# Another order of the pieces of an iteration in the chosen-token attention

## The chip, the core and the metric

The kernel runs on one core of one Trainium2 chip. The metric is the device time of one execution in microseconds. TensorE (PE) multiplies, VectorE (DVE), ScalarE (ACT) and GpSimd (POOL) do the elementwise work, and SyncE (SP) issues most of the plain DMAs. Each engine takes its instructions in a fixed order that is settled when the program is built, and waits on semaphores for the others.

## The reference

The reference is a chain of four blocks on x of shape (8, 512, 256) in float32, each added to its input: a gated recurrence with an MLP, a mixture of experts, a gated delta rule, and an attention among the half of the tokens that a gate chooses. The change is in the last one, which computes for every one of the eight batches:

```python
gate = jax.nn.sigmoid((token_inputs @ Wg)[..., 0])
_, idx = jax.lax.top_k(gate, C)                      # C = 256 of 512 tokens
attn_in = jnp.take_along_axis(token_inputs, idx[..., None], axis=1)
q, k, v = attn_in @ Wq, attn_in @ Wk, attn_in @ Wv   # 16 heads of 16
attn = jax.nn.softmax(jnp.einsum('bqhd,bkhd->bhqk', q, k) / jnp.sqrt(jnp.float32(dh)), axis=-1)
o = jnp.einsum('bhqk,bkhd->bqhd', attn, v).reshape(B, C, D) @ Wo
out = out.at[jnp.arange(B)[:, None], idx].set(o * gate_sel[..., None])
```

token_inputs is the layer-normalised x, and out is added to x.

## The kernel before

chosen_attention (from L1100) is a pipeline over the eight batches in 13 iterations. In iteration n seven parts work on seven different batches; a part is a generator, and every `yield` ends a piece of it.

- norm(n+1), one piece: loads x and normalises it to z.
- place(n), six pieces: turns z (ptd, L122), multiplies it by the gate's weights (pgt, L1167), and then on VectorE, token by token, counts how many gates lie ahead (L1181 to L1186): the rank. The last piece casts the rank to row numbers (L1189), scatters z with four indirect DMAs from GpSimd's queue (placed, L1193), one behind the other as all write one buffer, and loads the first 256 rows as c on SP's queue (L1195).
- project(n-1), six pieces: turns c (pct, copied to cT by VectorE at L1208), four pieces of products for q and k (pqk, L1220, two banks of 512 columns for each), and the products for v (pv, L1231).
- maxima(n-2), six pieces: for each half of the queries two pieces of scores (sc, L1250), whose negated row maxima VectorE takes (L1252), and one that turns the maxima (pmx, L1256) and adds them to q (L1257).
- sums(n-3), six pieces: for each half of the heads two pieces of scores of the other orientation (st, L1271), whose exponentials ScalarE takes (L1274), and one of products with v (po, L1281), copied to o (L1282).
- finish(n-4), five pieces: the denominators (pden, L1292, spread by GpSimd at L1297), two pieces that turn their reciprocals and multiply o (pr, L1304; L1305), the product with Wo (pdy, L1311, copied to y at L1312), and the DMAs: y stored on SP's queue (L1314), and read back row by row with four indirect DMAs from GpSimd's queue (got, L1317).
- leave(n-5), one piece: adds the gathered rows times the gate to x on VectorE (L1324, four instructions) and stores the result on SP's queue (L1325).

Every piece of scores, sc or st, takes all four banks of the pool px (the banks of scores), so it can start only when VectorE or ScalarE has read what the piece of scores before it left there. The other products use the pools pf and pp, two banks each:

```python
pf = cx.enter_context(tc.tile_pool(name="d_pf", bufs=2, space=PSUM))
pp = cx.enter_context(tc.tile_pool(name="d_pp", bufs=2, space=PSUM))
px = cx.enter_context(tc.tile_pool(name="d_px", bufs=4, space=PSUM))
```

The order of the pieces within an iteration is a list of letters written out by hand (L1338); what is left of a part is finished at the iteration's end. The tile framework then schedules: an instruction may be placed earlier or later on its engine than the list has it, even in a neighbouring iteration, as long as its inputs allow it, so that the list steers the engines' orders and does not fix them.

Of the kernel before, what the change touches and what calls it, by code (L numbers as in the profile page):

```python
# [45 lines left out]
def block(ctx: ExitStack, tc: tile.TileContext, a: dict, out: bass.AP):  # L46
# [1053 lines left out]
    def chosen_attention():  # L1100
# [4 lines left out]
        with ExitStack() as cx:  # L1105
# [45 lines left out]
            def norm(b):  # L1151
                x = tk.tile([P, NT, D], F32, name=f"dx{b}", tag="x", bufs=8)
                nc.sync.dma_start(x, rows_of(xbufs[1][b]))
                z = tk.tile([P, NT, D], F32, name=f"dz{b}", tag="z", bufs=3)
                center(sm, x, z, f"d{b}")
                zs[b] = x, z
                yield
# [170 lines left out]

            parts = {"p": (place, 0), "s": (sums, 3), "m": (maxima, 2), "q": (project, 1), "f": (finish, 4), "l": (leave, 5)}
            for _ in norm(0):
                pass
            for n in range(B + 5):
                at_work = {k: part(n - lag) for k, (part, lag) in parts.items() if 0 <= n - lag < B}
                if n + 1 < B:
                    at_work["n"] = norm(n + 1)
                for k in "p s q l m f p s q f m f s f p s q m q p s q m p m s q p m n f".split():  # L1338
                    if k in at_work:
                        next(at_work[k], None)  # L1340
                for left in at_work.values():
                    for _ in left:
                        pass

    chosen_attention()


# [44 lines left out]
```

## Time and profile before

| | |
|---|---|
| Time before, median of 3 runs | 3373.59 us (3373.55 to 3381.02) |
| The profiled execution's own time | 3381.53 us |
| Its span | 3379.8 us |
| TensorE busy in the span | 3018.4 us, 89% |
| VectorE | 1900.5 us, 56% |
| ScalarE | 1548.0 us, 46% |
| GpSimd | 574.0 us, 17% |
| DMA, mean | 90 GB/s |
| Granted TensorE clock, mean of the span | 0.91 |
| chosen_attention, in the span | 2904 to 3379.8 us |

The page reports one execution. A group's line has the source line, the engine, the operation, what it writes and reads, how often, the busy time and the mean of one, and at the end the idle time of its engine just before it and what ended it. The shares in the table are means over four blocks with different limits; the last block alone has TensorE busy 372.1 of its 476 us. The profiled execution is 7.9 us longer than the median of the runs.

### The profile page before, as it was taken

Reading aid. Unit: us, or ns where it says so; the run is one execution under the profiler, and the core shown is the slowest. Engines: PE = TensorE matmul, PEld = TensorE weight load, DVE = VectorE, ACT = ScalarE, POOL = GpSimd, SP = SyncE. Lnnn points to the kernel's source line nnn. Section 1 sums busy time; section 2 is a strip of 40 time slices with the busy share of each in tenths; the row PEclk is TensorE's granted clock in tenths of the full one; section 3 lists DMA queues with packets and bytes.
Section 4 is the critical chain, followed back from the end, with each engine's and each line's share of the span. In section 5 each row is a group of like instructions: output and inputs, shape, how many; then the busy total and the mean of one; then the engine's idle time right before and its main releaser. Section 6 shows DMA issues by size and latency. Waiting matters only on the chain.

```text
span 3379.8 us, 59439 instructions
## 1 busy us (share of the span) xinstructions
PE 3018.4 (89%) x24662; PEld 2227.4 (66%) x24662; DVE 1900.5 (56%) x4415; ACT 1548.0 (46%) x2747; POOL 574.0 (17%) x629
## 2 busy tenths in 40 slices
PE   7999999979999999977899898898989999498887
PEld 3655555535999999973566666666666667365664
DVE  4555545534555555556467767767677664554432
ACT  3554442212333333325466666767666663233322
POOL 1000001320000111014122222312121110212111
PEclk8999998989999999998789898989989896698787
DMA  5000003220788888871000000000000000201111
GB/s 205 13 25 13 13 13 148 69 67 19 271 337 330 330 327 320 327 284 31 2 1 20 8 20 8 26 2 26 2 23 2 8 2 8 94 23 42 36 40 47
DMA packets 97133, 302.69 MB, mean 90 GB/s; under 512 B 12760, under 2 KB 79456, under 8 KB 87648
## 3 DMA queue, kind: packets, MB, share of 16 engines
q0 software_dynamic: 19440, 221.19, 17.4%
q1 hardware_dynamic: 68016, 68.44, 6.0%
q10 hardware_dynamic: 9408, 9.27, 0.8%
q8 instruction: 194, 3.18, 0.4%
q14 instruction: 75, 0.61, 0.1%
HBM read 248.79 MB, written 50.08 MB: 88 GB/s over the span
## 4 chain that ended last, share of the span: by engine, by line
PE 69%; DVE 12%; DMA 11%; issue 4%; ACT 2%; POOL 2%; SPq 0%; another core or an unknown queue 0%; ACTq 0%; POOLq 0%; DVEq 0%
PE p_r L444 13%; PE pc L681 8%; DMA zbuf<-bz,rows 5%; PE pp L304 3%; PE pk L746 3%; PE pj L399 3%; PE pyr L522 3%; PE pkq L950 3%; DMA w<-in_experts,wrow 2%; PE pf L394 2%; PE p_s L444 2%; PE py L1008 2%; PE st L1271 2%; PE pw L957 1%; DVE cy L685 1%
## 5 line engine op out<-in xcount | busy, mean ns | idle before, releaser
L444 PE MATMUL p_r<-zT,w 128*128 128x128 f32 x4544 | 533.0, 275 | 6.1 <-DMA w<-in_experts,wrow 5.5
L444 PEld LDWEIGHTS p_r<-zT,w 128*128 128x128 f32 x4544 | 525.0, 192 | 11.6 <-issue 7.1
L685 DVE SCALAR_TENSOR_TENSOR cy<-pc,conv,cy 128x509 f32<-128x509 f32 (+2 forms) x480 | 351.4, 740 | 139.7 <-ACT cy L683 134.6
L448 ACT ACTIVATE t_r<-p_r,w 128x128 f32<-128x128 f32 x568 | 170.9, 374 | 263.5 <-PE p_r L444 183.9
L444 PE MATMUL p_s<-sxT,shared_w 128*128 128x512 f32 x512 | 226.2, 603 | 22.1 <-DVE l_s L449 20.4
L444 PEld LDWEIGHTS p_s<-sxT,shared_w 128*128 128x128 f32 x512 | 98.1, 193 | 145.6 <-issue 106.3
L508 POOL DMA_INDIRECT w<-in_experts,wrow x71 | 66.8, 940 | 676.3 <-ACT sg_r L457 655.8
L449 DVE SCALAR_TENSOR_TENSOR l_r<-p_r,w,t_r 128x128 f32<-128x128 f32 x284 | 80.0, 344 | 175.7 <-PE p_r L444 175.7
L681 PE MATMUL pc<-cxT,wq 128*128 128x512 f32 x256 | 150.8, 714 | 15.0 <-DVE cy L685 12.9
L681 PE MATMUL pc<-cxT,wk 128*128 128x512 f32 x256 | 146.0, 665 | 6.1 <-DVE cy L685 3.7
L304 PE MATMUL pp<-hT,win 128*128 128x512 f32 x320 | 142.9, 598 | 0.2 <-ACT hT L126 0.2
L522 PE MATMUL pyr<-w,htr 128*128 128x256 f32 x568 | 136.0, 383 | 2.6 <-DVE htr L462 2.6
L683 ACT ACTIVATE cy<-pc,conv 128x512 f32<-128x512 f32 x160 | 108.4, 686 | 62.3 <-PE pc L681 61.0
L449 DVE SCALAR_TENSOR_TENSOR g_r<-p_r,w,t_r 128x128 f32<-128x128 f32 x284 | 79.9, 344 | 98.8 <-PE p_r L444 98.8
L746 PE MATMUL pk<-kq 128*128 128x256 f32 x512 | 130.2, 391 | 0.7 <-DVE NQ L748 0.4
L728 POOL TENSOR_TENSOR e<-le,g 128x512 f32<-128x512 f32 x64 | 66.3, 1042 | 364.2 <-DVE NQ L748 341.6
L748 DVE SCALAR_TENSOR_TENSOR NQ<-pk,nbk,e 128x256 f32<-128x256 f32 x256 | 110.0, 477 | 27.2 <-PE pk L746 26.8
L394 PE MATMUL pf<-hT,fc 128*128 128x512 f32 x256 | 121.5, 601 | 0.0
L457 ACT ACTIVATE sg_r<-g_r 128x512 f32<-128x512 f32 x71 | 44.8, 631 | 159.9 <-DVE g_r L455 159.9
L399 PE MATMUL pj<-pj,sT 128*128 128x256 f32 x512 | 113.1, 379 | 0.0
L522 PEld LDWEIGHTS pyr<-w,htr 128*128 128x128 f32 x568 | 103.6, 192 | 14.2 <-issue 2.7
L950 PEld LDWEIGHTS pkq<-state,kq 128*128 128x128 f32 x768 | 95.4, 197 | 24.2 <-DVE state L972 16.7
(393 smaller groups left out, 6179.0 us busy)
## 6 DMA issues: line engine op xcount, KB each, us to landing
zt<-zbuf SPq DMA_DIRECT2D x71, 128.0 KB
ybuf<-yt SPq DMA_DIRECT2D x71, 128.0 KB
zbuf<-zeros SPq DMA_DIRECT2D x11, 768.0 KB
x<-in_x SPq DMA_DIRECT2D x8, 512.0 KB
xbuf<-x SPq DMA_DIRECT2D x8, 512.0 KB
sx<-xbuf SPq DMA_DIRECT2D x8, 512.0 KB
xbuf<-sx SPq DMA_DIRECT2D x8, 512.0 KB
cx<-xbuf SPq DMA_DIRECT2D x8, 512.0 KB
```

The source lines that it names most:

```text
L304: TE.matmul(ps, win[:, k, m : m + P], hT[:, k, :], start=k == 0, stop=k == DK - 1)
L394: TE.matmul(ps, fc[:, k, f * P : (f + 1) * P], hT2[:, k, :], start=k == 0, stop=k == DK - 1)
L399: TE.matmul(ps, sT[:, f, t * P : (t + 1) * P], pj[:, f, :], start=f == 0, stop=f == 7)
L444: last_of[0] = TE.matmul(ps[:, f, :], wx[:, k, (f0 + f) * P : (f0 + f + 1) * P], xin[:, k, :], start=k == 0, stop=k == DK - 1)
L448: S.activation(t3[:, f, :], p3[:, f, :], AF.Identity, bias=b3[:, f0 + f : f0 + f + 1])
L449: V.scalar_tensor_tensor(t1[:, f, :], p1[:, f, :], b1[:, f0 + f : f0 + f + 1], t3[:, f, :], ALU.add, ALU.mult)
L522: last_of[0] = TE.matmul(ps, hT[:, f, :], w2[:, f, :], start=f == 0, stop=f == 3)
L681: TE.matmul(ps, w[:, k, n * P : (n + 1) * P], xT[:, k, :], start=k == 0, stop=k == DK - 1)
L685: V.scalar_tensor_tensor(y[:, j:], ps[:, : T - j], conv[:, at + n, 3 - j : 4 - j], y[:, j:], ALU.mult, ALU.add)
L746: TE.matmul(pk[:, j, :, :], kq[:, h + j, 0, ts], kq[:, h + j, :, ts], start=True, stop=True)
L748: V.scalar_tensor_tensor(NQ[:, :, t * HG + h + j, :], pk[:, j, :, :], s.nbk[:, t, h + j : h + j + 1], bc(e[:, h + j, :], 1, 2), ALU.mult, ...
L950: TE.matmul(ps[:, n, h, :], s.kq[:, h, n, ts], state[:, h, :], start=True, stop=True)
```

## The change

Only the list of letters changes (an added empty line above it moves the later lines by one). It has the same letters but for one q more: project has six pieces, and a seventh call finds it finished.

```diff
             for n in range(B + 5):
                 at_work = {k: part(n - lag) for k, (part, lag) in parts.items() if 0 <= n - lag < B}
                 if n + 1 < B:
                     at_work["n"] = norm(n + 1)
-                for k in "p s q l m f p s q f m f s f p s q m q p s q m p m s q p m n f".split():
+                for k in "p s q q m f q s f q p m f s s p m f s q p m n l q m p s q p m f".split():
                     if k in at_work:
                         next(at_work[k], None)
```

By the list, l (the adding of results) moves from the fourth place to the 24th, n (the norm) from the 30th to the 23rd, the pieces of project move forward, and between two pieces that use the banks of scores (m and s, other than their third and sixth pieces) stand other pieces with products: two q between the first s and the first m, f and q between that m and the next s, and so on. Place's second piece comes after four pieces of project. Finish's fourth piece (f, pdy) comes after the fourth piece of sums and the third of maxima.

## The prediction

> **What bounds the kernel now.** I read the waits of the last stage first, then the stage cut into its iterations, then one iteration in order of time. The change touches only chosen_attention, which runs from 2904 us to the end, 476 of 3379.8 us.
>
> The waits from 2904 us on (engine, line, what is waited for: total us, times, longest):
>
> ```profile
> DVE dx L1324 <- DMA got<-result,at: 104.2, 30, 14.8
> ...
> POOL got L1317 <- DMA result<-dy: 90.1, 7, 23.2
> ...
> PE sc L1250 <- DVE maxs L1252: 30.1, 8, 8.3
> ```
>
> VectorE stands 104.2 us in front of the additions of leave, until the gathers land; TensorE stands 30.1 us because VectorE has not released score banks. The stage in stretches from one gate product (pgt) to the next: the two starting iterations, iterations 4 to 7, then 8 and 9, which place nothing (columns: stretch, length, busy us of PE, PEld, DVE, ACT, POOL, then granted clock):
>
> ```profile
> 2952.00:3032.60 80.60, 71.90 (x439) 49.96 (x439) 45.04 (x105) 26.60 (x48) 12.00 (x12) 0.89 0.09 29
> 3032.60:3088.80 56.20, 46.03 (x298) 31.70 (x297) 23.65 (x52) 17.36 (x31) 10.22 (x11) 0.79 0.13 38
> ...
> 3140.90:3191.60 50.70, 44.60 (x297) 31.52 (x296) 22.45 (x48) 17.37 (x31) 10.28 (x11) 0.80 0.14 42
> ...
> 3240.90:3285.80 44.90, 41.45 (x288) 29.51 (x285) 15.31 (x26) 13.23 (x27) 4.98 (x6) 0.81 0.10 30
> 3285.80:3325.90 40.10, 34.15 (x242) 22.79 (x240) 14.87 (x26) 10.50 (x21) 4.97 (x6) 0.74 0.11 34
> ```
>
> TensorE is busy 44.6 of 50.7 us at a clock of 0.80, so it is not at its own limit. What sets the 50.7 us is in the iteration from 3140.9, in order of time:
>
> ```profile
> 3148.78 0.69 DVE L1252 TENSOR_REDUCE maxs<-sc 128x2 f32<-128x512 f32 x1
> ...
> 3156.62 0.17 DVE L1189 CAST at<-rank 128x4 int32<-128x4 f32 x1
> ...
> 3157.07 1.06 POOL L1193 DMA_INDIRECT placed<-dz,at  x1 [7.20 <-DVE rank L1190]
> ...
> 3165.23 0.97 POOL L1193 DMA_INDIRECT placed<-dz,at  x1 [1.73 <-DMA placed<-dz,at]
> ...
> 3167.69 0.36 SPq L1195 DMA_DIRECT2D c<-placed  x1
> ...
> 3168.09 0.47 SPq L1314 DMA_DIRECT2D result<-dy  x1
> ...
> 3172.00 0.98 POOL L1317 DMA_INDIRECT got<-result,at  x1 [5.80 <-DMA result<-dy]
> ...
> 3175.14 0.48 DVE L1324 SCALAR_TENSOR_TENSOR dx<-got,col,dx 128x256 f32<-128x256 f32 x1 [12.77 <-DMA got<-result,at]
> ...
> 3180.08 3.86 PE L1250 MATMUL sc<-dk,dq 32*128 32x256 f32 x16 [4.38 <-DVE maxs L1252]
> ...
> 3187.44 2.23 PE L1231 MATMUL pv<-mwv,cT 128*128 128x256 f32 x8
> ```
>
> That is a loop: gate product, rank on VectorE (done 3156.8), four scatters one behind the other (10.6 us), the load of c on SP's queue and the store of y behind it (0.4 us later, though y was copied by 3166.8), four gathers, four additions, the reductions behind them, the fourth piece of maxima's scores (3180.08), the last po, pv, and the next gate product at 3191.62. Whatever lies on it counts in full; whatever TensorE does between the gate product and 3175.7 lies beside it.
>
> **The change, part by part.** No instruction is added or removed[...]. I count from the order in which the two built programs place instructions, engine by engine.
>
> *Adding of results.* In the list l moves from place 4 to 24. In the built order it does not move against what matters: the additions of batch n-4 still stand on VectorE between the second half of finish and the reductions of the third maxima scores, in the iteration that gathers them. Only the add of maxima's negated maxima (dq, 0.68 us) now goes wholly before them. So the 12.77 us stay, and SP's queue (c, y, out) and POOL's (scatters, gathers) keep their order. In iteration 9 alone the order differs: one addition, then the four reductions, then the other three. Cost of the move: 0; what covers it is the gather, which is later than everything else. Without that cover an addition would cost 0.48 us.
>
> *v product (pv).* It goes from behind the last po, on the loop, to before the fourth maxima scores, where TensorE idles 4.06 to 8.34 us for VectorE. In the four placing iterations it took, up to the next transpose, 2.48, 1.83, 2.07 and 2.34 us, mean 2.2. Gain 2.2 a round. Against that, the transposes behind the last po (0.43 + 1.05 us) now come 2.2 us earlier after the idle stretch, when the clock may still be half; half the cases double a part of them: +0.4.
>
> *q and k products.* The first q product (pqk) now comes behind only one of the four first maxima banks. Its first reduction on VectorE keeps its time, as both halves of bank 0 go ahead of the product. The other three banks follow it. The product starts when cT is copied (7.46 us after the gate product), takes 3.4 us at half clock, and bank 1 is reducible 1.2 to 2.0 us later: 11.9 to 13.0. VectorE, which in the new order does six small rank operations before those three reductions, would be there at 11.4. So rank, and with it the scatters, come 0.2 to 1.65 us later, by the state of the clock; I take 1.0.
>
> Here the row and a rule differ. In the Trainium skill, "TensorE: Matmul & The Clock Gate", Part 1 (the HAM clock gate), the clock falls to half after an idle window of about 3.4 us and returns after a busy one. The granted clock (third column from the end) in such stretches:
>
> ```profile
> 3143.50:3146.90 3.40, 2.80 (x31) 2.38 (x24) 0.67 (x1) 3.36 (x5) 1.26 (x1) 1.00 0.00 0
> 3146.90:3150.30 3.40, 3.40 (x18) 2.91 (x18) 3.25 (x10) 1.33 (x3) 1.17 (x2) 0.51 0.00 0
> ...
> 3153.70:3157.10 3.40, 3.40 (x10) 2.22 (x9) 3.19 (x10) 1.58 (x4) 0.03 (x1) 0.50 0.00 0
> ```
>
> TensorE was busy 2.80 of 3.40 us and lost the clock all the same: much of it is pden, 16 products of 4 columns. By the rule as worded the moved product would run at full clock and the delay be 0, 4 us less over four rounds; the row says half clock, and I use it. The return agrees with the rule: dense pqk brought it back at 3157.
>
> *y product (pdy)* moves behind the first scores of sums' second half and a transposition, and two pqk products now also precede it: 1.99 + 1.89 + 1.15 + 0.60 = 5.6 us more before it at full clock; but three gated score pieces that waited for banks no longer wait. Walking TensorE in the new order with the durations above, y is copied 27.4 to 28.3 us after the gate product; the scatters let c go at 26.8 + (0.2 to 1.65), y's store 0.4 later. So y is in time, with 0 to 0.6 us to spare.
>
> Sum of a placing iteration: -2.2 + 0.4 + 1.0 = -0.8; four of them: -3.2 (between -7 and +4).
>
> *Iteration 8* has products to spread but no scatters, so y's store sets the loop. Before, pden and a wait of 0.73 us cost the clock from 3245.9 to 3256, and pdy ended 23.7 us after the transposes. In the new order a dense pqk stands in that window; at full clock pdy ends at 21.5. Gain 2.0, plus pv's 1.8, less 0.6 for a chance of losing the clock: -3.2. *Iteration 9*: pdy comes 1.4 later, but the first reduction waits for one gather instead of four (3313.38 against 3317.21): -2.4. *The tail*: pdy and a score piece change places, -0.5 at most.
>
> *The start* (iterations 2 and 3): rank 2 loses 1.9 us to reductions, its scatters hold the load of c and the normalisation behind them, and the next scores of sums wait some 3 us; then the gate products win pv's 1.9 and the spread products some more. By the same walk, between -2 and +3; I take -1.
>
> Sum: -3.2 - 3.2 - 2.4 - 0.5 - 1 = -10.3 us. The profiled execution took 3381.5 us (span 3379.8 and 1.7 around it), so it would be 3371; the runs shown have the median 3373.6, so 3363.
>
> **The rivals.** *Gain given back (3371.5):* the three banks come the full 1.65 us late and the transposes behind po all meet half clock (+1.1 with part of the gate product): a round is then +0.5, four +2, iteration 8 -1.8, 9 -2.4, start 0: -2. For it: every iteration before falls to half clock for about 10 us twice. Against: the moved products are dense, which is what brought the clock back.
>
> *Slower (3389): y late.* If the clock stays half from the first q product until pdy, as it did for 10.2 us from 3146.9, three windows of 3.4 us cost 1.7 each, 5.1 us before y's copy, with no more than 0.6 spare. It decides from the point where y's copy is later than the issue of c. A round is then +4.3, four +17, iteration 8 +2, the rest -3.4: about +16. For it: five and a half us of work were put ahead of y. Against: pqk at 3153.7 restored the clock within one window.
>
> *Clock never lost (3358):* the denser order keeps the clock through the first product, delay 0 and y early: four rounds less 1.2 each. Against: pden and the wait for ScalarE's exponentials stay ahead of it.
>
> **How the numbers follow.** The main case 0.60, own range 3356 to 3371; gain given back 0.20; y late 0.15; clock never lost 0.05. About 0.3% (10 us) is what a measurement of this kernel can tell from no change. The main case lies on that bound: 0.40 of it faster, 0.20 the same. Faster by over 0.3%: 0.40 + 0.05 = 0.45. Within: 0.20 + 0.20 + 0.02 = 0.42. Slower: 0.13. Range 3353 to 3382; beyond lie most of y late and a small gain in excess.
>
> **What would show it.** Right: gate products 50 us apart or less in iterations 5 to 7; dx still waiting some 12 us; pv inside the idle stretch; the cast of rank 0.2 to 1.7 us later after its gate product; the store of y 0.4 us behind c; iteration 8 some 3 us shorter. Wrong: a store of y over 1 us behind the issue of c, a rank over 2 us later, additions that no longer stand before the reductions, or any gain outside the last stage.

## The result, and the profile after

The changed kernel takes 3358.49 us (median of 4 runs, 3357.35 to 3359.55) beside 3375.74 us before on the same chip: the ratio is 0.9948, with a 95% interval of 0.9933 to 0.9964. That is 17 us faster; the prediction had 10 us, with 3363 us inside 3353 to 3382. A second measurement of the same order of instructions on another chip (l_back, below) gave 12 us, so 12 to 17 us is what is known of the gain. The profiled execution took 3359.55 us, with a span of 3357.8 us in place of 3379.8.

The waits of the last stage, after (engine, line, what is waited for: total us, times, longest):

```profile
DVE dx L1324 <- DMA got<-result,at: 103.8, 28, 16.0
...
PE sc L1250 <- DVE maxs L1252: 41.3, 6, 10.1
```

VectorE still stands 103.8 us in front of the additions. The loop that set the iteration before sets it after, and moving the letter l has not taken the wait away. TensorE's wait for banks has grown from 30.1 to 41.3 us: work was taken out of the loop and put ahead of that wait.

The stage in the same stretches as before, from iteration 4 on (stretch, length, busy us of PE, PEld, DVE, ACT, POOL, then granted clock):

```profile
3028.00:3079.70 51.70, 40.58 (x297) 28.11 (x296) 23.99 (x52) 17.33 (x31) 10.23 (x11) 0.83 0.14 42
...
3129.90:3178.80 48.90, 40.49 (x297) 27.92 (x296) 22.70 (x48) 17.36 (x31) 10.26 (x11) 0.86 0.15 44
...
3227.30:3268.20 40.90, 35.69 (x286) 25.46 (x284) 15.39 (x26) 13.01 (x25) 4.97 (x6) 0.87 0.11 33
3268.20:3306.90 38.70, 33.75 (x243) 22.85 (x241) 14.63 (x26) 10.12 (x19) 4.98 (x6) 0.69 0.10 30
```

TensorE's busy time in iteration 6 falls from 44.60 to 40.49 us for the same instructions, and the clock rises from 0.80 to 0.86; yet the iteration is only 1.8 us shorter. Most of TensorE's gain lies beside the loop. The same iteration in order of time (its gate product starts at 3129.92):

```profile
3137.39 2.78 PE L1220 MATMUL pqk_True<-cT,mwq 128*128 128x256 f32 x8 [0.42 <-DVE cT L1208]
...
3142.12 1.89 DVE L1252 TENSOR_REDUCE maxs<-sc 128x2 f32<-128x512 f32 x3 [0.86 <-PE sc L1250]
...
3146.59 0.17 DVE L1189 CAST at<-rank 128x4 int32<-128x4 f32 x1
...
3156.34 0.58 ACT L1312 COPY dy<-pdy 128x512 f32<-128x512 f32 x1 [2.09 <-PE pdy L1311]
...
3157.66 0.36 SPq L1195 DMA_DIRECT2D c<-placed  x1
3158.07 0.90 SPq L1314 DMA_DIRECT2D result<-dy  x1
...
3160.63 1.99 PE L1231 MATMUL pv<-mwv,cT 128*128 128x256 f32 x8
...
3165.07 0.48 DVE L1324 SCALAR_TENSOR_TENSOR dx<-got,col,dx 128x256 f32<-128x256 f32 x1 [11.50 <-DMA got<-result,at]
...
3170.01 3.86 PE L1250 MATMUL sc<-dk,dq 32*128 32x256 f32 x16 [7.39 <-DVE maxs L1252]
```

The first q product stands at 7.47 us after the gate product, the three other banks are read from 12.2 us on (the x3 row), and the cast of rank comes at 16.67 us (15.73 before). pv is over at 3162.6, and then TensorE stands idle 7.39 us until VectorE, held by the gathers, frees a bank. From the fourth scores to the next gate product (3178.81) it is now 8.80 us, not 11.54.

The granted clock in stretches of that iteration (third column from the end):

```profile
3135.00:3138.40 3.40, 2.38 (x12) 1.73 (x12) 3.03 (x8) 2.25 (x5) 0.89 (x3) 1.00 0.00 0
3138.50:3141.80 3.30, 3.30 (x17) 1.98 (x15) 2.75 (x9) 0.60 (x1) 0.40 (x1) 0.50 0.00 0
...
3165.90:3176.00 10.10, 5.99 (x40) 3.80 (x44) 6.33 (x11) 0.00 (x0) 0.81 (x1) 0.50 0.26 78
```

The half clock after pden is still there, but for 3.4 us, not 10.2 as before (3146.9 to 3157.1), and the dense q product falls into it. In l_back, the same order of instructions, the four placing iterations have 6.8 and 3.4 us by turns, in the two profiles of the old order 10.2 or 13.6. The second spell, some 10 us behind the idle stretch, is as long as before, and the fourth scores lie in it: 3.86 us.

### The profile page after: what moved, and what is told of

The parts are those of the page before. It is cut to its first block, busy times and chain, and to the rows that moved or that the text cites. A ratio compares the mean times of both kernels' runs of the same rounds, so it can differ in the third digit from the quotient of the medians.

```text
span 3357.8 us, 59439 instructions
## 1 busy us (share of the span) xinstructions
PE 2982.0 (89%) x24662; PEld 2197.4 (65%) x24662; DVE 1901.4 (57%) x4415; ACT 1546.2 (46%) x2747; POOL 574.7 (17%) x629
## 4 chain that ended last, share of the span: by engine, by line
PE 38%; DVE 9%; DMA 3%; issue 3%; ACT 2%; POOL 1%; SPq 0%; POOLq 0%; DVEq 0%; ACTq 0%
PE pc L681 8%; PE pk L746 3%; PE pkq L950 3%; PE py L1008 2%; PE pw L957 1%; PE sc L1250 1%; PE st L1271 1%; PE pg L924 1%; DVE cy L685 1%; PE pow L976 1%; PE po L1281 1%; PE pn L876 1%; PE pu L885 1%; PE pqk_True L1220 1%; PE pn L701 1%
## 5 line engine op out<-in xcount | busy, mean ns | idle before, releaser
L728 POOL TENSOR_TENSOR e<-le,g 128x512 f32<-128x512 f32 x64 | 66.2, 1040 | 363.2 <-DVE NQ L748 340.5
```

## The experiments

Every kernel differs from the one before, or from the changed one, by its list or by the few lines shown. The time of the last stage in the profiled execution (first gate product to the end of the span) sorts them better than the total, as the stages ahead are the same in all and their end varies by 14 us from profile to profile (2910.8 to 2924.4). "4 to 7" is the sum of the four placing iterations, from gate product to gate product; iteration 8 has none, so iteration 7 ends with the transposes of c (pct) of iteration 8. "sc" are the scores of maxima, four pieces in each iteration.

| kernel | q, k products | pv | additions | ratio to before (95%) | last stage, us | 4 to 7 |
|---|---|---|---|---|---|---|
| before | as before | behind po | before the reductions | 1 | 455.4 | 208.3 |
| l_only | as before | behind po | same | 1.0006 (0.9996 to 1.0016) | 452.2 | 205.4 |
| pv_only | as before | ahead of 4th sc | same | 0.9941 (0.9922 to 0.9960) | 434.7 | 195.4 |
| pv_back | between banks | behind po | same | 1.0012 (1.0005 to 1.0019) | 451.8 | 209.3 |
| after | between banks | ahead of 4th sc | same | 0.9948 (0.9933 to 0.9964) | 435.5 | 199.3 |
| l_back | between banks | ahead of 4th sc | same | 0.9966 (0.9957 to 0.9975) | 436.1 | 200.9 |
| q_late | between banks, but the first q behind all of the 1st sc | ahead of 4th sc | same | 0.9960 (0.9947 to 0.9974) | 434.3 | 196.0 |
| late_before | as before | behind po | behind the reductions | 0.9931 (0.9916 to 0.9946) | 427.9 | 186.2 |
| late_pv | as before | ahead of 4th sc | behind the reductions | 0.9869 (0.9854 to 0.9885) | 408.0 | 173.7 |
| late_after | between banks | ahead of 4th sc | behind the reductions | 0.9804 (0.9789 to 0.9819) | 383.5 | 159.3 |
| late_q_late | between banks, but the first q behind all of the 1st sc | ahead of 4th sc | behind the reductions | 0.9806 (0.9790 to 0.9823) | 385.3 | 159.4 |
| pool_add | between banks | ahead of 4th sc | on GpSimd | 0.9813 (0.9797 to 0.9829) | 393.3 | 164.0 |

### l_only and l_back: the additions' letter alone

```diff
 l_only, against before
-"p s q l m f p s q f m f s f p s q m q p s q m p m s q p m n f"
+"p s q m f p s q f m f s f p s q m q p s q m p m s q p m n l f"
 l_back, against after
-"p s q q m f q s f q p m f s s p m f s q p m n l q m p s q p m f"
+"p s q l q m f q s f q p m f s s p m f s q p m n q m p s q p m f"
```

> The kernel before with one change of the three: the letter of the additions moved from the fourth place to near the end (between the next batch's normalization and the last finishing piece); banks and the value projection as before. Theory of the gather loop (the additions' place among VectorE's instructions is unchanged in iterations 5 to 8, so the move is worth nothing there, and only iteration 9 can gain, at most 2.4 us): 3371 to 3376 us, ratio 0.9988 to 1.000. Rival (the additions' move is the source of the gain): ratio 0.995 to 0.997, 3359 to 3366 us.

> The changed kernel with the letter of the additions put back at the fourth place; banks and the value projection as changed. Theory of the gather loop: like the changed kernel, 0 to +2.5 us (only iteration 9), 3358 to 3361 us, ratio to the kernel before 0.9948 to 0.9958. Rival (the additions' move is the source): close to the kernel before, ratio 0.998 to 1.000.

Measured: 3374.97 us for l_only (ratio 1.0006) and 3361.70 for l_back (0.9966), both ratios a little above what was expected; the rival, that the letter brings the gain, falls. The built programs show why: l_only has the order of the kernel before, and l_back that of the changed kernel, instruction for instruction on all five engines. The letter does nothing at all, in iteration 9 either, where the forecast for these two runs still allowed a gain. l_back is therefore the changed kernel measured again, with 22 runs beside 51 of the kernel before: 12 us, not 17. And each of the two orders has two profiles, which show what chance does: 455.4 and 452.2 us for the stage, 435.5 and 436.1. Iteration 4 took 56.23 us in one and 53.86 in the other profile of the very same order before. The gain of the change, mean against mean, is 18.0 us of the stage.

### pv_only and pv_back: the value projection alone

```diff
 pv_only, against before: the last product of project ahead of the fourth scores
-"p s q l m f p s q f m f s f p s q m q p s q m p m s q p m n f"
+"p s q l m f p s q f m f s f p s q m q p s q m q p m s p m n f"
 pv_back, against after: the same product behind the last po
-"p s q q m f q s f q p m f s s p m f s q p m n l q m p s q p m f"
+"p s q q m f q s f q p m f s s p m f s q p m n l m p s q q p m f"
```

> The kernel before with the last product of the projection (the value projection) moved ahead of the fourth maxima scores, and nothing else. Theory (the value projection stands on the loop between the fourth scores and the next gate product; ahead of them it lies in TensorE's wait for the gathers): -2.2 us in each of iterations 4 to 8 and at the start -2, no delay of the rank: -9 to -14 us, 3362 to 3367 us, ratio 0.9958 to 0.9973; from the fourth scores to the next gate product 8.5 to 9.5 us in place of 10.2 to 12.0; the rank cast 15.6 to 15.7 us after its gate product as before. Rival (the products between the banks' uses bring the gain through a better clock or earlier scores): within 3 us of the kernel before.

> The changed kernel with the value projection put back behind the last of the weighted sums. Theory: the loop grows by 2.2 us in each of iterations 4 to 8, +9 to +14 us on the changed kernel, while the rank stays 1.0 us late: 3367 to 3373 us, ratio to the kernel before 0.9975 to 1.0005. Rival (banks and additions bring the gain): like the changed kernel, ratio 0.995. If the odd scatter landings of the kernel before (1.8 and 2.2 us in iterations 4 and 5) belong to its order they stay away here, and the time is 4 us below the kernel before.

Measured: pv_only 3355.21 us, ratio 0.9941, as good as the whole change or better; pv_back 3376.70 us, 1.0012, which is 15 us above l_back on the same chip where 9 to 14 were expected. The rival, that the products between the banks bring the gain, falls: without pv's move they bring none. In the stage, pv's move is worth 453.8 - 434.7 = 19 us in the old order (453.8 is the mean of before and l_only), and 451.8 - 435.8 = 16 us in the new one. In pv_back's iteration 6 the old place is to be seen (its next gate product follows at 3191.75):

```profile
3179.74 3.86 PE L1250 MATMUL sc<-dk,dq 32*128 32x256 f32 x16 [9.29 <-DVE maxs L1252]
...
3187.10 2.70 PE L1231 MATMUL pv<-mwv,cT 128*128 128x256 f32 x8
```

TensorE idles 9.29 us in front of the fourth scores, and then pv's 2.70 us stand between po and the next gate product. From the fourth scores to the next gate product it takes 9.9 to 12.0 us there (iterations 4 to 7), mean 10.8; in after and l_back the mean is 8.9.

pv_only won 5 to 10 us more than was expected of it. Part of it is in its fourth scores (iterations 5 and 7):

```profile
3121.08 2.92 PE L1250 MATMUL sc<-dk,dq 32*128 32x256 f32 x16 [1.35 <-DVE maxs L1252]
...
3217.46 3.05 PE L1250 MATMUL sc<-dk,dq 32*128 32x256 f32 x16 [2.20 <-DVE maxs L1252]
```

In its order the third scores come late (33.6 to 34.7 us after the gate product in iterations 5 to 7; 29.3 in the changed kernel), so that pv directly behind them fills the idle stretch down to 1.35 and 2.20 us. The granted clock stays at 1.0 to 3134.8 in the one and to 3220.1 in the other, past the scores or nearly, and they take 2.92 and 3.05 us, not 3.86; from their start to the next gate product it is 6.95 and 6.84 us. In iterations 4 and 6 it is 9.95 and 10.04. The mean falls from 11.1 (l_only) to 8.4. A short idle stretch alone does not secure the clock: in iteration 6 it is 2.10 us, no longer than in iteration 7, and the clock still falls, at 3168.9, in the middle of the fourth scores.

### q_late: the first q product back behind the first scores

```diff
 against after
-"p s q q m f q s f q p m f s s p m f s q p m n l q m p s q p m f"
+"p s q m f q q s f q p m f s s p m f s q p m n l q m p s q p m f"
```

> The changed kernel with its first q product put back behind all four banks of the first maxima scores; the value projection ahead of the fourth scores, and all else, as changed. Theory (the product between the banks makes the rank 1.0 us late, and the rank is on the loop in iterations 4 to 7): the cast of rank 15.6 to 15.8 us after its gate product in place of 16.7, -4 us on the changed kernel, ratio to the kernel before 0.9935 to 0.9955. Rival (the product between the banks costs nothing, the loop being set elsewhere): like the changed kernel, ratio 0.9948 to 0.9966.

Measured: 3354.58 us, ratio 0.9960 (0.9947 to 0.9974). By the ratio it can't be told from the changed kernel, 0.9948 to 0.9966; that is where the rival put it, though the interval reaches into the theory's range. The trace says more. In its iteration 5 (gate product at 3070.59), and at the start of its iteration 8 (last row):

```profile
3079.99 1.88 DVE L1252 TENSOR_REDUCE maxs<-sc 128x2 f32<-128x512 f32 x3
...
3086.17 0.17 DVE L1189 CAST at<-rank 128x4 int32<-128x4 f32 x1
...
3098.30 0.59 ACT L1312 COPY dy<-pdy 128x512 f32<-128x512 f32 x1 [2.09 <-PE pdy L1311]
3098.40 0.36 SPq L1195 DMA_DIRECT2D c<-placed  x1
3098.91 0.36 SPq L1314 DMA_DIRECT2D result<-dy  x1
...
3223.37 6.19 PE L1220 MATMUL pqk_True<-cT,mwq 128*128 128x256 f32 x16
```

The three reductions start at 9.4 us instead of 12.2 and the cast stands at 15.58: the delay of 1.0 us is the place of that product, as forecast. But the time won on the rank does not reach the gathers. y is copied only 28.3 us after the gate product, later than c is issued (27.8), so now y itself decides when its store is issued. In iterations 4, 5 and 7 that store stands at 28.2 to 28.3 us, within 0.2 us of its place in the changed kernel's profile; only in iteration 6 is it 0.8 us earlier. Iterations 4 to 7 together take 196.0 us against 199.3 and 200.9, which is as much as was expected; yet iterations 5 and 6 are shorter by no more than 0.5 us, the rest lies in 4 and 7 and was not traced, and two profiles of one order differ by 2.9 us in this sum (208.3 and 205.4). So this run does not show what an earlier rank is worth. Iteration 8 is back at 44.83 us (44.9 before, 40.9 after). That loss is the other half of the same edit: the q products start 7.5 us after the transposes of c and not 3.3, the clock is at half again from 3221.6 to 3228.4, and the two take 6.19 us together (in the changed kernel 1.99 us each at full clock). pdy ends 25.9 us after the transposes, in the changed kernel 21.2, and the gain that the prediction gave to iteration 8 is gone.

### late_before, late_pv, late_after: is it the gather wait that sets the iteration?

```diff
 def leave(b):
     x, col, got = gots.pop(b)
+    late = sm.tile([P, NT], F32, name=f"late{b}", tag="late")
+    V.scalar_tensor_tensor(late, maxs[1][:, 0, :, 16], 0.0, col, ALU.mult, ALU.add)
     for t in range(NT):
-        V.scalar_tensor_tensor(x[:, t, :], got[:, t, :], col[:, t : t + 1], x[:, t, :], ALU.mult, ALU.add)
+        V.scalar_tensor_tensor(x[:, t, :], got[:, t, :], late[:, t : t + 1], x[:, t, :], ALU.mult, ALU.add)
```

late_after has the list of the changed kernel; late_before and late_pv have those of before and of pv_only with l behind the fourth m.

> The changed kernel with the four additions of leave bound to a place behind the reductions of the third maxima scores: their scalars pass through one more VectorE instruction (128x4) that adds 0 times those maxima, so the additions of a batch stand one iteration later and find their gathers landed. Theory (the gather wait on VectorE, 11.5 to 12 us in front of the additions, holds the fourth maxima scores and so sets the iteration): the fourth scores come right behind the value projection, 33 us after the gate product in place of 40.2; iterations 4 to 8 are 5 to 8 us shorter each, 3318 to 3332 us, ratio 0.983 to 0.988. Rival (TensorE at its half clock or the scatter chain is the next bound and keeps the iteration): at most 2 us an iteration, 3348 us or more, ratio over 0.992.

> The kernel before with the value projection ahead of the fourth scores and, as in the kernel late_after, the additions bound behind the third maxima's reductions. Here the q and k products stand after whole sets of banks, and the third maxima scores come 33.6 us after the gate product, not 29.3. Theory (with the gather wait gone TensorE's own order sets the iteration, and the bank order of the change is worth its 4.3 us): the fourth scores at 37 us, iterations 3 us shorter than with the value projection alone, 3338 to 3346 us, slower than late_after by 12 to 22 us. Rival (the order between the banks is worth nothing or costs its 1.0 us a round in any case): equal to late_after or 2 to 4 us below it.

> The kernel before with only the additions bound behind the third maxima's reductions, as in late_after. Theory: the fourth scores come 35.5 us after the gate product in place of 39 to 41, and the value projection behind the last po now costs its full time again as TensorE has no idle stretch: iterations of 45 us, 3346 to 3354 us. Rival (the wait for the gathers is not what sets the iteration before): within 5 us of the kernel before.

Measured: 3305.64, 3327.51 and 3345.88 us. All are below what was expected or at its lower end, in the order that the theory of the gather wait gave; the rivals fall. The fourth scores start where they were expected, 32.6 to 35.4 us after the gate product in late_after and 36.8 to 37.9 in late_pv. late_after is 66 us faster than before, nearly four times the gain of the change. Its waits of the last stage, and its iteration 6 in order of time (gate product at 3104.99):

```profile
DVE dx L1326 <- DMA got<-result,at: 31.1, 8, 15.4
...
PEld sc L1250 <- DVE maxs L1252: 3.0, 8, 0.7
```

```profile
3136.85 1.99 PE L1231 MATMUL pv<-mwv,cT 128*128 128x256 f32 x8
...
3138.78 1.51 PE L1250 MATMUL sc<-dk,dq 32*128 32x256 f32 x16
...
3139.34 1.67 DVE L1326 SCALAR_TENSOR_TENSOR dx<-got,late,dx 128x256 f32<-128x256 f32 x4
...
3140.93 2.48 DVE L1252 TENSOR_REDUCE maxs<-sc 128x2 f32<-128x512 f32 x4
3142.15 0.96 POOL L1317 DMA_INDIRECT got<-result,at  x1 [0.30 <-issue]
```

The fourth scores follow pv at once, find all four banks free and run at full clock: 1.51 us, not 3.86. (Not all of the 2.35 us is the clock's. In the changed kernel the scores start as soon as the first bank is free and then go at the pace of the reductions; in pv_only they do so at full clock and take 2.92 us.) The four additions, of rows gathered an iteration earlier, take 1.67 us in one row; the last gather of this iteration is issued only at 3142.15 and nobody waits for it here. What is left of VectorE's waiting for gathers, 31.1 us, lies in the last batches. TensorE is busy almost throughout:

```profile
3104.99:3145.33 40.34, 38.80 (x298) 26.99 (x297) 22.68 (x49) 17.36 (x31) 10.55 (x11) 0.92 0.20 57
```

So the wait cost three times: 7.4 us idle, scores that went at the pace of the reductions, and the clock behind it. The columns of the table also show what the bank order of the change is worth: with the additions in the way nothing (452 to 454 us of the stage without pv's move, 435 to 436 with it, in either order), with them out of the way 408.0 - 383.5 = 24 us. The new order has the third scores ready some 4 us sooner, and only kernels with the additions out of the way can use that.

### late_q_late and pool_add: two counter-tests

late_q_late is late_after with the list of q_late. pool_add is the changed kernel with

```diff
-    for t in range(NT):
-        V.scalar_tensor_tensor(x[:, t, :], got[:, t, :], col[:, t : t + 1], x[:, t, :], ALU.mult, ALU.add)
+    G.tensor_mul(got, got, bc(col, 2, D))
+    G.tensor_add(x, x, got)
```

> The kernel late_after with the first q product behind all four first maxima banks, as in q_late. In q_late that brought the rank 1.0 us forward and each iteration 0.8 us down. Theory (the rank counts only as long as the gather wait holds the fourth scores; with the additions out of the way TensorE's order sets the iteration): the cast of rank at 15.6 us, yet no gain, 0 to +1.3 us an iteration since the third maxima scores come 1.3 us later, 3304 to 3312 us, ratio 0.980 to 0.983. Rival (the rank stands on the path in any order): 3 to 5 us below late_after, ratio 0.9785 or less.

> The changed kernel with the additions of leave taken from VectorE's queue in another way: two GpSimd instructions on 128x1024 (multiplication by col, then addition) in place of four on VectorE, nothing else. Theory (what counts is only that no reduction stands behind the gathers): the fourth scores at 33 us as in late_after; the two instructions take about 2.5 us each by the 1.26 us of GpSimd's 128x512, end some 5 us behind the last gather and hold the next diagonal dg by 0 to 2 us: 3305 to 3325 us, ratio 0.980 to 0.987. Rival (the gain of late_after comes from the later place of the additions in the iteration or of the stores of out on SP's queue, not from the gather wait): 3340 us or more, ratio over 0.990.

Measured: late_q_late 3311.73 us, ratio 0.9806, not distinguishable from late_after's 0.9804, though its cast of rank came at 15.6 to 16.4 us and not at 16.7 to 17.8. With the additions out of the way an earlier rank brings nothing. pool_add took 3313.85 us, ratio 0.9813: the gain comes from freeing VectorE's queue, whichever way it is done. On GpSimd's queue, around the next gate product (3105.01):

```profile
3104.98 1.89 POOL L1323 TENSOR_TENSOR got<-got,col 128x1024 f32<-128x1024 f32 x1 [2.38 <-DMA got<-result,at]
3106.95 2.34 POOL L1324 TENSOR_TENSOR dx<-dx,got 128x1024 f32<-128x1024 f32 x1
3110.22 1.26 POOL L1171 TENSOR_TENSOR dg<-row,ident 128x512 f32<-128x512 f32 x1 [0.93 <-ACT row L1169]
```

The two instructions end at 3109.29 and dg still waits 0.93 us for ScalarE's row, so here they do not hold it. In the iteration before they do: dg starts right behind them, 1.9 us after its row was ready, within the 0 to 2 us that were expected, and the cast of rank comes at 18.95 us after the gate product. The last stage is 10 us longer than late_after's; the totals, on two chips, do not differ.

## Why the prediction was right, point by point

The main case came, at 17 us (12 in l_back) instead of 10. The median, 3358.5 us, is also the number of the rival "clock never lost" (3358), but the trace speaks against that one: a half clock behind pden of 3.4 or 6.8 us stands in every placing iteration of after and l_back, and the rank is late. In the means of two profiles for each order (before and l_only; after and l_back):

| term of the sum | forecast | measured |
|---|---|---|
| iterations 2 and 3 | -1 | -3.2 (66.2 to 63.0) |
| iterations 4 to 7 | -3.2 | -6.8 (206.9 to 200.1) |
| iteration 8 | -3.2 | -4.0 (44.9 to 40.9) |
| iteration 9 | -2.4 | -1.5 (40.2 to 38.7) |
| tail | -0.5 | -2.6 (53.4 to 50.8) |

*The loop* was read rightly: dx still waits 103.8 us, y's store stands 0.41 us behind c, and the additions stand before the reductions. (Only the stretch of the start was cut wrongly: 2952.0 is no gate product. From that of iteration 2 to that of iteration 4 it was 65.1 us, not 80.6; the table has it so.) That it is the loop was argued from one trace; late_before, late_after and pool_add show it.

*The additions' letter at 0* is right, and more so than stated. Iteration 9's other order of additions and reductions comes with the bank order, not with l: l_back has it (38.65 us), and pv_only hasn't (41.18).

*pv off the loop:* 2.2 us a round were read from the trace, less 0.4 for a colder clock. Measured from the fourth scores to the next gate product: 11.2 us before, 8.9 after, -2.3. The deduction of 0.4 was not needed.

*The rank later by 1.0:* in the old order the casts of iterations 4 to 7 stand at 15.57 to 15.85 us, after at 16.66 to 16.69, in l_back at 16.52 to 17.80: mean against mean 1.2 (16.9 for 15.7), within the 0.2 to 1.65 that were given, though iteration 4 of l_back alone is 2.1 later than the old mean. The delay does reach y's store: in iterations 6 and 7 it stands at 27.2 us in the old order and at 28.1 to 29.0 in the new one. The prediction had set a row of the granted clock against the rule of the Trainium skill ("TensorE: Matmul & The Clock Gate", Part 1) and went by the row. The row held, by half: the q product met the half clock from 3138.4 to 3141.8, but its first microsecond was at full clock, and it took 2.78 us, not 3.4. That the return of the clock agrees with the rule was too much said. By the prediction's own rows TensorE was busy 3.40 of 3.40 us from 3146.9 to 3150.3, with scores, and the clock stayed at half to 3157.1.

*y in time:* y was copied at 3156.92, c issued at 3157.66: 0.74 us to spare, forecast 0 to 0.6. The rival that y is late needed a half clock up to pdy; in this iteration it ended 3.4 us after it began.

*Iteration 8* came as forecast and for the reason given: a dense q product now stands in the window after pden, no half clock shows from 3227 to 3258, and pdy ends 21.2 us after the transposes (forecast 21.5, before 23.7); from the fourth scores to the next pden it takes 8.2 us, before 9.6. pv_back, without pv's move, has pdy at the same 21.2, and where the product is put back (q_late) the gain is lost. But gains don't add there: pv_only alone won 4.1 us, pv_back alone 3.0, both together 4.0. In pv_only the half clock behind pden is still there; the one behind the fourth scores is gone instead.

*What was mis-sized* is the start and the tail, 5.8 us for 1.5. In the tail, a piece of sums' scores that changes places with pdy was given 0.5 us; from iteration 10's pden to iteration 11's it brought 1.5 (26.1 us in both profiles of the old order, 24.6 in both of the new), as the last exponentials could begin before pdy. The rest of the tail and the 2.2 us of the start were not taken apart; in the start the two profiles of the old order alone differ by 2.1 us. Of iterations 4 to 7, -2.3 and +1.2 a round give -4.4. The remaining -2.4 lies in the scatters: from the cast of rank to the issue of c it is 11.1 to 11.4 us in the new order's two profiles, but 12.6 to 13.3 in three of the old order's eight iterations, where one scatter landed late. Whether the order has a part in that is not shown: pv_back has no such landing, late_after has one. So a part of the excess over the forecast is luck, as far as these runs show.

The prediction had no term for an idle stretch that costs the clock for what follows it. It counted pv's own time, though pv's place also decides how long TensorE idles in front of the next scores, and the clock that they get. Iterations 5 and 7 of pv_only show such a gain (6.9 us from the scores to the gate product, where 4 and 6 have 10.0); its iteration 6, with as short a stretch and the clock lost, shows that it does not come every time.

## What to carry to other kernels

Find the instruction that waits longest in an in-order queue and ask what stands behind it: here four additions of no urgency, waiting for gathers, held the reductions that free TensorE's banks, and taking them out of that place brought some 49 us (ratio 0.9804 beside 0.9948) on top of the reordering. Where a list only steers a scheduler, compare the built order before costing a moved letter: this one moved no instruction, and a dependency on the late result did what the list could not. An edit that makes something ready earlier is worth nothing in front of a longer wait and may be worth much once that wait is gone: the bank order brought 0 us here, and 24 us behind the other edit.

## What the runs showed of the hardware

- The granted clock fell to half without an idle window: TensorE was busy 2.38 us of 3.40 (3135.00 to 3138.40, the last part of pden, gated scores and the start of a q product) and lost it; the next 3.3 us, busy throughout with dense products among them, regained it. Busy time alone did not decide: before the change 3.40 us of 3.40, filled with scores (3146.9 to 3150.3), did not bring the clock back.
- Behind an idle stretch of 7.4 us the clock was at half for some 10 us. The 16 score products behind it took 3.86 us; at full clock, but still waiting for one bank after the other, 2.92; at full clock with all banks free, 1.51.
- A scatter in the chain of four took 2.7 us from issue to issue (16.18 to 18.94 us after the gate product in iteration 6 before); single ones landed some 2 us later.
- Two GpSimd instructions on 128x1024 float32 took 1.89 (product with a broadcast column) and 2.34 us (sum), beside 4 x 0.48 us for the same work fused on VectorE.
- Two builds with the same order of instructions differed by 3.2 us of the last stage in their profiles before and by 0.6 us after: single profiles of this kernel tell no less than 3 us apart.
